# End of the spectral ffn: the last back-transform with two places at a time in the two halves of TensorE's array

## The chip, the cores and the metric

The kernel runs on one core of a Trainium2 chip. Its time is device microseconds of one execution. The kernel before was timed three times: 2250.99, 2252.79 and 2252.90 us, median 2252.79 us. The profile shows one such execution, with a span of 2251.2 us and a mean granted TensorE clock of 0.991.

## The reference, cut to what matters

The program computes two layers on a feature map `x` of 2 batches, 128 channels and 64 x 64 positions. Layer 0 is neighbourhood attention with a small feed-forward part. Layer 1 is global attention over 4096 tokens, and then a spectral ffn with a residual. The change lies at the very end of that ffn:

```python
def _stu_conv(phi, u, n):                     # causal convolution with K = 16 filters
    U_plus = irfft(Vf[None, :, :, None] * rfft(u)[:, :, None, :])[:, :sl]
    ...
def _compute_spectral(u, sigma, phi, Mpp, Mpm):
    out = einsum('btkd,k,kde->bte', U_plus, s, Mpp)
    out = out + einsum('btkd,k,kde->bte', U_minus, s, Mpm)
...
t = t + _L1_ffn_ref(_ln_t(t), ...)            # the residual
x = _from_tokens(t, x)                        # output: batch, channel, position
```

The kernel does the convolutions block by block in a frequency domain. At the end the spectrum of each result must go back to positions, and the residual `t` must be added.

## The kernel before, in words

Everything is float32. The ffn uses blocks of 256 positions; a block's transform has 320 real coefficients, which are 160 bins of 2 (`BINS` = 160). For each group of `GB` = 4 bins, `group()` multiplies inputs with filters (L1299: a contraction of 64 rows, alternately in rows 0 to 63 and 64 to 127 of the array, copied out by VectorE and ScalarE at L1300). `project()` contracts the result with 32 matrices of 128 x 128 (L1311), and ScalarE copies the finished accumulator to the spectrum tile `ob` (L1317). There are 40 such groups.

`ob` has channels on its partitions. Along the free dimension it has parity (2), batch (2), place `f` inside a stride of 8 (`FB` = 8), bin (160) and real or imaginary part (2). A "place" here is one combination of batch, parity and `f`: 2 x 2 x 8 = 32 places. The way back to positions takes each place apart:

- The bins are cut into chunks of 64, 64 and 32, so a chunk has 128, 128 and 64 coefficients.
- `turn()` transposes a place's coefficients by TensorE into PSUM (L1327, tile `pt`), so that coefficients lie on partitions, and ScalarE copies them to `t` (L1329).
- `back()` multiplies them with the inverse transform `inv` (L1338, tile `py`), contracting over the coefficients: 128 rows for chunks 0 and 1, 64 rows for chunk 2.
- For chunks 0 and 1, `back_into()` adds the result to `xa`, the residual in channel-major layout, by VectorE (L1350). These steps are slipped between the projections of later groups: TensorE's order in that loop is written by hand (`manual_schedule`).
- Chunk 2 is complete only after the last group, so it is done behind the loop. A list `last` holds 16 entries: half `h` of the positions, batch, parity and four places starting at `f0`. For each entry TensorE does four transposes and four back-multiplications, one entry's transposes ahead of the previous entry's multiplication, and VectorE adds `xa` and writes the output tile `o` (L1386). Each `o` holds one batch and one half of the positions, 1 MB; it is stored by one DMA of the sync queue (L1390). There are four, and `o` has two buffers.

The two halves `h` use the same coefficients with different columns of `inv`, so in this version every place is transposed twice. All PSUM tiles of this part (`pc`, `pt`, `py`) come from one ring of six buffers, `ps_c`.

Of the kernel before, what the change touches and what calls it, by code (L numbers as in the profile page):

```python
# [8 lines left out]
F32 = mybir.dt.float32  # L9
AF = mybir.ActivationFunctionType  # L10
ALU = mybir.AluOpType
# [3 lines left out]
P = 128  # L15
NB = 2
T = 4096
TH = T // 2
# [62 lines left out]
CB, FB, SG = 256, 8, 4  # L81
SB = CB // SG
NC = CB + SB

CHUNKS = (0, 1, 4, 5, 2, 3, 6, 7)
BINS = NC // 2
GB = 4
LG = 2 * FB
GROW = 4 * LG * KF


@with_exitstack
def kernel(
# [16 lines left out]
    nc = tc.nc  # L110
# [12 lines left out]
    xa = [xp.tile([P, T], F32, tag=f"xa{b}", name=f"xa{b}") for b in range(NB)]  # L123
# [15 lines left out]
    ident = const.tile([P, P], F32, name="ident")  # L139
# [79 lines left out]
    with l0a:  # L219
# [64 lines left out]
        for r in range(QT):  # L284
            lo = 6 - min(r, 6)
            src = bass.AP(
                rpb_pad.tensor, (RPR + r - 6) * RPW + 50, [[1, QT], [RPW, (HEADS - 1) * RPR - r // 7], [1, NTAB]]
            )
            rows_ = rev[r * QT : (r + 1) * QT].rearrange("p h n m -> p (h n) m")
# [979 lines left out]
    with ExitStack() as cv:  # L1269
        cp = cv.enter_context(tc.tile_pool(name="conv", bufs=5))  # L1270
        obp = cv.enter_context(tc.tile_pool(name="ob", bufs=1))
        ps_c = cv.enter_context(tc.tile_pool(name="ps_c", bufs=6, space=PSUM))
        ps_p = cv.enter_context(tc.tile_pool(name="ps_p", bufs=2, space=PSUM))

        ob = obp.tile([P, 2, NB, FB, BINS, 2], F32, name="ob")

        def inputs(q):

            ut = cp.tile([P, NB, 2, P], F32, tag="ut", name="ut")
            nc.sync.dma_start(  # L1280
                out=ut.rearrange("p b s d -> p (b s d)"),
                in_=us[2 * q : 2 * q + 2].rearrange("g i r f b s d -> (g i r f) (b s d)"),
            )
            return ut

        def group():


            y = cp.tile([P, 8, KF, 2, 32], F32, tag="y", name="y", bufs=2)
            for q in range(GB // 2):  # L1290
                ct, ut = ahead.pop(0)
                for par in range(2):

                    cv_ = ct[:, :, 0 : 288 + par * 32].rearrange("p o (l c) -> p o l c", l=2)[:, :, :, 0 : FB * KF]
                    for b in range(NB):
                        for f in range(2):
                            fp = slice(f * 64, (f + 1) * 64)
                            pc = ps_c.tile([P, 2, 2, FB * KF], F32, tag="pc", name="pc")
                            nc.tensor.matmul(pc, lhsT=ut[fp, b, par, :], rhs=cv_[fp], start=True, stop=True)  # L1299
                            (nc.scalar.copy if f else nc.vector.tensor_copy)(  # L1300
                                y[:, 4 * f : 4 * f + 4, :, par, b * 2 * FB + q : (b + 1) * 2 * FB : 2],
                                pc.rearrange("p r l (t k) -> p (r l) k t", k=KF),
                            )
                if to_load:
                    q_ = to_load.pop(0)
                    ahead.append((blocks(q_), inputs(q_)))
            return y

        def project(g, y, acc, l, k):

            nc.tensor.matmul(  # L1311
                acc, lhsT=(mmi if l else mpl)[:, k, :], rhs=y[:, 1::2, k, ::-1, :] if l else y[:, 0::2, k, :, :],
                start=(l == 0 and k == 0), stop=(l == 1 and k == KF - 1),
            )
            if l == 1 and k == KF - 1:
                ov = ob.rearrange("p s b t g r -> p (s b t) (g r)")[:, :, g * GB * 2 : (g + 1) * GB * 2]
                nc.scalar.copy(  # L1317
                    ov.rearrange("p m (q x) -> p x m q", q=2), acc.rearrange("p (x m q) -> p x m q", x=4, q=2)
                )

        def turn(chunk, b, par, f0, n):

            bn = min(64, BINS - chunk * 64)
            pt = ps_c.tile([P, n, P], F32, tag="pc", name="pt")
            for j in range(n):
                src = ob[:, par, b, FB - 1 - f0 - j, chunk * 64 : chunk * 64 + bn, :]
                nc.tensor.transpose(pt[0 : 2 * bn, j, :], src.rearrange("p g r -> p (g r)"), ident)  # L1327
            t = cp.tile([P, 4, P], F32, tag="t", name="t", bufs=2)
            nc.scalar.copy(t[0 : 2 * bn, 0:n, :], pt[0 : 2 * bn])  # L1329
            return t  # L1330

        def back(chunk, t, n, h):

            bn = min(64, BINS - chunk * 64)
            c0, cn = (0, CB) if h is None else (h * P, P)
            py = ps_c.tile([P, n, cn], F32, tag="pc", name="py")
            for j in range(n):
                nc.tensor.matmul(  # L1338
                    py[:, j, :], lhsT=t[0 : 2 * bn, j, :], rhs=inv[0 : 2 * bn, chunk, c0 : c0 + cn],
                    start=True, stop=True,  # L1340
                )
            return py

        def back_into(chunk, b, par, f0):

            t = turn(chunk, b, par, f0, 2)
            yield True
            py = back(chunk, t, 2, None)
            xv = xa[b][:, par * TH : (par + 1) * TH].rearrange("p (h f c) -> p f h c", h=2, f=FB)[:, f0 : f0 + 2]
            nc.vector.tensor_tensor(xv, py.rearrange("p f (h c) -> p f h c", h=2), xv, ALU.add)  # L1350
            yield None

        places = [(b, par, f0) for b in range(NB) for par in range(2) for f0 in range(0, FB, 2)]
        to_load = list(range(BINS // 2))
        ahead = [(ct, inputs(to_load.pop(0))) for ct in first_blocks]
        rest = []
        with tc.manual_schedule(engines={mybir.EngineType.PE}):
            y = group()
            for g in range(BINS // GB):
                following = group() if g + 1 < BINS // GB else None  # L1360
                acc = ps_p.tile([P, 64 * GB], F32, tag="acc", name="acc")
                for l in range(2):
                    for k in range(KF):
                        project(g, y, acc, l, k)
                        if rest and k in ((3, 11) if g >= 128 // GB else (7,)):
                            if next(rest[0], None) is None:
                                rest.pop(0)
                y = following
                if (g + 1) * GB in (64, 128):
                    rest += [back_into(g * GB // 64, *p) for p in places]  # L1370
            for steps in rest:
                for _ in steps:
                    pass


        last = [(h, b, par, f0) for h in range(2) for b in range(NB) for par in range(2) for f0 in range(0, FB, 4)]
        ahead = [turn(2, *last[0][1:], 4)]
        for i, (h, b, par, f0) in enumerate(last):
            if i + 1 < len(last):
                ahead.append(turn(2, *last[i + 1][1:], 4))  # L1380
            if par == 0 and f0 == 0:
                o = cp.tile([P, P, FB, 2], F32, tag="o", name="o", bufs=2)
            xv = xa[b][:, par * TH + h * (TH // 2) : par * TH + (h + 1) * (TH // 2)]
            xv = xv.rearrange("p (f c) -> p c f", f=FB)
            py = back(2, ahead.pop(0), 4, h)
            nc.vector.tensor_tensor(  # L1386
                o[:, :, f0 : f0 + 4, par], py.rearrange("p f c -> p c f"), xv[:, :, f0 : f0 + 4], ALU.add
            )
            if par == 1 and f0 + 4 == FB:
                nc.sync.dma_start(out=outf[b, :, h * TH : (h + 1) * TH], in_=o.rearrange("p c f r -> p (c f r)"))  # L1390


# [19 lines left out]
def _transforms():  # L1412

    import numpy as np

    f = np.arange(BINS)[None, :]
    real = (f == 0)

    def parts(n):
        n = np.arange(n)[:, None]
        a = 2 * np.pi * ((f * n) % NC) / NC
        return np.cos(a), -np.sin(a), (1.0 - 2.0 * (n % 2)) + 0.0 * f

    def pack(*cols):
        return np.stack(cols, axis=-1).reshape(cols[0].shape[0], -1).astype(np.float32)

    c, m, alt = parts(SB)
    seg = pack(c, np.where(real, alt, m))  # L1430
    c, m, alt = parts(CB)
    filters = pack(c, np.where(real, 0.0, m), np.where(real, 0.0, -m), np.where(real, alt, c))
    back = np.zeros((3 * P, CB), np.float32)
    back[0:NC] = pack(np.where(real, 1.0, 2.0 * c) / NC, np.where(real, alt, 2.0 * m) / NC).T
    return np.concatenate([seg, seg]), filters, back


# [49 lines left out]
```

## Time and profile before

| what | value |
|---|---|
| median time | 2252.79 us |
| span of the profile | 2251.2 us |
| TensorE busy | 2183.3 us, 97% of the span |
| VectorE busy | 939.8 us, 42% |
| ScalarE busy | 783.8 us, 35% |
| last projection ends, last projection copied out | 2217.7 us, 2218.3 us |
| last VectorE addition ends | 2245.9 us |
| transposes in the tail (128 x 64 weights) | 64, 279 ns each |
| back-multiplications in the tail (64 x 128 weights) | 128 instructions, 284 ns each |
| additions in the tail (L1386) | 16, 1042 ns each |

A matmul in float32 appears as two instructions in the trace, so the 64 calls of `back()`'s matmul in the tail are 128 instructions; a transpose is one. [...]consecutive instructions overlap. So the distance from start to start, which the chain of waits shows as time per group, is what an instruction costs TensorE, and the mean duration is not.

"64*128" after a TensorE instruction is the part of the array that its weights fill: 64 rows and 128 columns.

### The profile page before, as it was taken

The numbers are of one execution on the slowest core, as the hardware profiler recorded it, in microseconds if no ns is written. First come the engines' busy times: TensorE is split into PE (matmuls) and PEld (weight loads), VectorE is DVE, ScalarE is ACT, GpSimd is POOL, SyncE is SP. The second block draws the span as 40 slices with busy tenths as digits, with TensorE's granted clock in tenths as the row PEclk, the third lists the DMA queues.
The fourth block names the chain that finished last, engine by engine and source line by source line (L and its number), as shares of the span: only waits on it lengthen the run. The fifth ranks groups of instructions, "written<-read, shape, count | busy, mean of one in ns | idle before, by whom it ended". The sixth has DMA issues, their size and how long they took to land.

```text
span 2251.2 us, 31746 instructions
## 1 busy us (share of the span) xinstructions
PE 2183.3 (97%) x11908; PEld 1352.2 (60%) x11908; DVE 939.8 (42%) x3047; ACT 783.8 (35%) x1911; POOL 276.8 (12%) x354
## 2 busy tenths in 40 slices
PE   5899998999999999999999999999999999999998
PEld 3677765544445444444544447677677776767677
DVE  4799985433344336533233342222222323232323
ACT  2789883222333233222222332322322223232322
POOL 3367874200000000000000000000000000000000
PEclk8999998999999999999999999999999999999999
DMA  4222213011100016100000122212212122221101
GB/s 115 67 62 61 61 52 51 0 47 61 38 24 6 19 47 177 43 24 10 15 24 24 47 84 64 53 44 58 54 44 58 40 57 44 54 50 47 43 7 75
DMA packets 180858, 109.76 MB, mean 49 GB/s; under 512 B 32225, under 2 KB 165857, under 8 KB 180194
## 3 DMA queue, kind: packets, MB, share of 16 engines
q1 hardware_dynamic: 177866, 105.47, 17.9%
q10 hardware_dynamic: 2840, 2.27, 0.4%
q8 instruction: 94, 1.54, 0.3%
q14 instruction: 58, 0.48, 0.1%
HBM read 73.09 MB, written 34.60 MB: 48 GB/s over the span
## 4 chain that ended last, share of the span: by engine, by line
PE 85%; DVE 6%; POOL 3%; DMA 3%; ACT 1%; issue 1%; SPq 1%; DVEq 0%; ACTq 0%; POOLq 0%
PE acc L1311 25%; PE pc L1299 13%; PE bank L896 9%; PE own L924 9%; PE other L949 8%; PE bank L910 4%; PE py L1338 2%; PE bank L331 2%; PE bank L188 2%; PE bank L541 1%; PE bank L1041 1%; PE bank L1009 1%; PE bank L1150 1%; DMA st<-in_m_minus_dram 1%; PE po L563 1%
## 5 line engine op out<-in xcount | busy, mean ns | idle before, releaser
L1300 DVE COPY y<-pc 128x512 f32<-128x512 f32 x320 | 221.5, 692 | 351.5 <-PE pc L1299 347.8
L903 ACT ACTIVATE e<-bank 128x512 f32<-128x512 f32 x288 | 171.9, 597 | 558.9 <-PE bank L896 426.6
L896 PE MATMUL bank<-cm 128*128 128x512 f32 x576 | 298.4, 602 | 1.4 <-DVE y L652 1.4
L1311 PE MATMUL acc<-y,mpl 128*128 128x256 f32 x1280 | 292.1, 382 | 0.0
L1311 PE MATMUL acc<-y,mmi 128*128 128x256 f32 x1280 | 288.0, 379 | 0.0
L1299 PE MATMUL pc<-ct,ut 64*128 64x512 f32 x1280 | 285.2, 595 | 0.9 <-issue 0.9
L1311 PEld LDWEIGHTS acc<-y,mpl 128*128 128x128 f32 x1280 | 238.1, 190 | 59.4 <-issue 29.6
L1311 PEld LDWEIGHTS acc<-y,mmi 128*128 128x128 f32 x1280 | 242.6, 190 | 32.7
L1300 ACT COPY y<-pc 128x512 f32<-128x512 f32 x320 | 204.3, 638 | 87.4 <-PE pc L1299 87.4
L924 PE MATMUL own<-et,tok 128*128 128x512 f32 x448 | 227.2, 594 | 1.9 <-DVE part L913 1.9
L949 PE MATMUL other<-e,tok 128*128 128x512 f32 x448 | 228.6, 592 | 0.0
L913 DVE CUSTOM_DVE_ANT_0 et<-bank,one 128x512 f32<-128x512 f32 x224 | 145.7, 688 | 166.7 <-PE bank L910 166.6
L1299 PEld LDWEIGHTS pc<-ct,ut 64*128 64x128 f32 x1280 | 121.5, 187 | 145.8 <-issue 140.6
L1317 ACT COPY ob<-acc 128x256 f32<-128x256 f32 x40 | 23.8, 595 | 431.2 <-PE acc L1311 431.2
L924 PEld LDWEIGHTS own<-et,tok 128*128 128x128 f32 x448 | 84.3, 190 | 110.4 <-issue 72.4
L949 PEld LDWEIGHTS other<-e,tok 128*128 128x128 f32 x448 | 85.0, 190 | 106.6 <-issue 106.2
L896 PEld LDWEIGHTS bank<-cm 128*128 128x128 f32 x576 | 96.5, 193 | 73.3 <-issue 44.9
L1350 DVE TENSOR_TENSOR xa<-py,xa 128x512 f32<-128x512 f32 x32 | 22.2, 692 | 281.4 <-PE py L1338 281.4
L910 PEld LDWEIGHTS bank<-ident,e 128*128 128x128 f32 x896 | 103.4, 141 | 55.1 <-issue 47.2
L160 POOL TENSOR_TENSOR ln_rs<-ln_rs,mhalf 128x4 f32<-128x4 f32 x24 | 24.3, 1010 | 857.8 <-DVE ln_rs L159 857.8
L528 ACT ACTIVATE p<-p,mn 128x196 f32<-128x196 f32 x256 | 114.4, 449 | 21.6 <-DVE mn L518 13.9
L910 PE MATMUL bank<-ident,e 128*128 128x128 f32 x896 | 116.9, 273 | 0.0
(200 smaller groups left out, 2335.7 us busy)
## 6 DMA issues: line engine op xcount, KB each, us to landing
ut<-us SPq DMA_DIRECT2D x80, 256.0 KB
us<-ub SPq DMA_DIRECT2D x64, 256.0 KB
vw<-vd SPq DMA_DIRECT2D x256, 49.0 KB
ct<-gs SPq DMA_DIRECT2D x160, 72.0 KB
ct<-gs SPq DMA_DIRECT2D x160, 64.0 KB
gs<-ub SPq DMA_DIRECT2D x20, 256.0 KB
vd<-v SPq DMA_DIRECT2D x128, 32.0 KB
st<-in_m_plus_dram SPq DMA_DIRECT2D x16, 256.0 KB
```

Source lines behind the costliest of these rows:

```text
L188: nc.tensor.transpose(ps[:, j * P : (j + 1) * P], src[:, j, :], ident)
L331: nc.tensor.matmul(pl, lhsT=wg[:, lo : lo + P], rhs=zT, start=True, stop=True)
L528: nc.scalar.activation(p, p, AF.Exp, bias=t[name + "mn"][:, h : h + 1], scale=-1.0, accum_out=t["den"][:, u, h : h + 1],)
L896: nc.tensor.matmul(ps, lhsT=cm[b][:, n * P : (n + 1) * P], rhs=cm[b][:, chunk(c)], start=True, stop=True)
L903: nc.scalar.activation(e, ps, AF.Exp, bias=0.0, scale=ASCALE, accum_out=part[:, n, c : c + 1])
L910: nc.tensor.transpose(pt[:, k * P : (k + 1) * P], es[k][:, m * P : (m + 1) * P], ident)
L913: nc.vector.tensor_tensor_reduce(et, pt, one, 1.0, 0.0, ALU.mult, ALU.add, part[:, n, a : a + 1])
L924: nc.tensor.matmul(own, lhsT=tok[b][:, n, :], rhs=e, start=first, stop=last)
L949: nc.tensor.matmul(other, lhsT=tok[b][:, 4 * CHUNKS[a] + j, :], rhs=es[j], start=(j == 0), stop=(j == 3))
L1299: nc.tensor.matmul(pc, lhsT=ut[fp, b, par, :], rhs=cv_[fp], start=True, stop=True)
L1300: (nc.scalar.copy if f else nc.vector.tensor_copy)(y[:, 4 * f : 4 * f + 4, :, par, b * 2 * FB + q : (b + 1) * 2 * FB : 2], pc.rearrange("p ...
L1311: nc.tensor.matmul(acc, lhsT=(mmi if l else mpl)[:, k, :], rhs=y[:, 1::2, k, ::-1, :] if l else y[:, 0::2, k, :, :], start=(l == 0 and k = ...
```

## The change

The chunk of 64 coefficients fills only half of the array's rows. The change puts the transposed coefficients of two places into one tile, one place in rows 0 to 63 and the other in rows 64 to 127, and multiplies both at the same time, each in its half of the array.

- The last 32 bins get a spectrum tile of their own, `ob_last`, in which two neighbouring places lie side by side: 2 x 32 x 2 = 128 contiguous numbers. One transpose of 128 x 128 turns two places. All 16 transposes run ahead of the multiplications, once, and both halves `h` use their results; four `t` tiles hold them, so `t` gets four buffers where it had two.
- The rows of `inv` for chunk 2 are stored twice, so that rows 64 to 127 hold the same matrix as rows 0 to 63.
- The multiplications alternate between the two halves of the array, into two PSUM tiles, `odd` and `even`.
- For the even places TensorE also adds the residual: a multiplication of `xa` with the identity matrix starts the accumulation, and ScalarE copies the sum to `o`. For the odd places VectorE adds the residual as before.
- `turn()` and `back()` are folded into `back_into()`, which does for chunks 0 and 1 what it did.

```diff
-        ob = obp.tile([P, 2, NB, FB, BINS, 2], F32, name="ob")
+        ob = obp.tile([P, 2, NB, FB, 2 * BC, 2], F32, name="ob")
+        ob_last = obp.tile([P, 2, NB, FB, BINS - 2 * BC, 2], F32, name="ob_last")
...
-                ov = ob.rearrange("p s b t g r -> p (s b t) (g r)")[:, :, g * GB * 2 : (g + 1) * GB * 2]
+                o_, g0 = (ob, g * GB) if g * GB < 2 * BC else (ob_last, g * GB - 2 * BC)
+                ov = o_.rearrange("p s b t g r -> p (s b t) (g r)")[:, :, g0 * 2 : (g0 + GB) * 2]
...
-            t = cp.tile([P, 4, P], F32, tag="t", name="t", bufs=2)
+            t = cp.tile([P, 4, P], F32, tag="t", name="t", bufs=4)
...
-        last = [(h, b, par, f0) for h in range(2) for b in range(NB) for par in range(2) for f0 in range(0, FB, 4)]
-        ahead = [turn(2, *last[0][1:], 4)]
-        for i, (h, b, par, f0) in enumerate(last):
-            if i + 1 < len(last):
-                ahead.append(turn(2, *last[i + 1][1:], 4))
...
-            py = back(2, ahead.pop(0), 4, h)
-            nc.vector.tensor_tensor(
-                o[:, :, f0 : f0 + 4, par], py.rearrange("p f c -> p c f"), xv[:, :, f0 : f0 + 4], ALU.add
-            )
+        turned_ = {}
+        for b in range(NB):
+            for par in range(2):
+                pt = ps_c.tile([P, 4, P], F32, tag="pc", name="pt")
+                for i in range(4):
+                    src = ob_last[:, par, b, 2 * i : 2 * i + 2]
+                    nc.tensor.transpose(pt[:, 3 - i, :], src.rearrange("p m g r -> p (m g r)"), ident)
+                turned_[b, par] = cp.tile([P, 4, P], F32, tag="t", name="t", bufs=4)
+                nc.scalar.copy(turned_[b, par], pt)
+        for h in range(2):
+            for b in range(NB):
+                o = cp.tile([P, P, FB, 2], F32, tag="o", name="o", bufs=2)
+                for par in range(2):
...
+                    odd, even = (ps_c.tile([P, 4, P], F32, tag="pc", name="py") for _ in range(2))
+                    nc.tensor.matmul(even, lhsT=ident, rhs=xv[:, 0::2], start=True, stop=False)
+                    for i in range(4):
+                        for q, py in ((0, odd), (1, even)):
+                            rows_ = slice(q * 64, (q + 1) * 64)
+                            nc.tensor.matmul(
+                                py[:, i, :], lhsT=turned_[b, par][rows_, i, :], rhs=inv[rows_, 2, h * P : (h + 1) * P],
+                                start=(q == 0), stop=(q == 0 or i == 3),
+                            )
+                    nc.scalar.copy(o[:, :, 0::2, par], even.rearrange("p f c -> p c f"))
+                    nc.vector.tensor_tensor(
+                        o[:, :, 1::2, par], odd.rearrange("p f c -> p c f"), xv[:, 1::2].rearrange("p f c -> p c f"), ALU.add
+                    )
                 nc.sync.dma_start(out=outf[b, :, h * TH : (h + 1) * TH], in_=o.rearrange("p c f r -> p (c f r)"))
...
+    back[NC:] = back[2 * P : NC]
```

More of the change, by code (lines that the diff above doesn't have):

```diff
@@ L87 @@
 GB = 4
+BC = 64
 LG = 2 * FB
@@ L1319, in project @@
                 )
[L1321 to L1327, printed above, removed]
-            t = cp.tile([P, 4, P], F32, tag="t", name="t", bufs=2)
[L1329 to L1340, printed above, removed]
-                )
-            return py
-        def back_into(chunk, b, par, f0):
-            t = turn(chunk, b, par, f0, 2)
+        def back_into(chunk, b, par, f0):
+            pt = ps_c.tile([P, 2, P], F32, tag="pc", name="pt")
+            for j in range(2):
+                src = ob[:, par, b, FB - 1 - f0 - j, chunk * BC : (chunk + 1) * BC, :]
+                nc.tensor.transpose(pt[:, j, :], src.rearrange("p g r -> p (g r)"), ident)
+            t = cp.tile([P, 4, P], F32, tag="t", name="t", bufs=4)
+            nc.scalar.copy(t[:, 0:2, :], pt)
             yield True
-            py = back(chunk, t, 2, None)
+            py = ps_c.tile([P, 2, CB], F32, tag="pc", name="py")
+            for j in range(2):
+                nc.tensor.matmul(py[:, j, :], lhsT=t[:, j, :], rhs=inv[:, chunk, :], start=True, stop=True)
             xv = xa[b][:, par * TH : (par + 1) * TH].rearrange("p (h f c) -> p f h c", h=2, f=FB)[:, f0 : f0 + 2]
@@ L1364 @@
                         project(g, y, acc, l, k)
-                        if rest and k in ((3, 11) if g >= 128 // GB else (7,)):
+                        if rest and k in ((3, 11) if g >= 2 * BC // GB else (7,)):
                             if next(rest[0], None) is None:
@@ L1368 @@
                 y = following
-                if (g + 1) * GB in (64, 128):
-                    rest += [back_into(g * GB // 64, *p) for p in places]
+                if (g + 1) * GB in (BC, 2 * BC):
+                    rest += [back_into(g * GB // BC, *p) for p in places]
             for steps in rest:
@@ L1373 @@
                     pass
-        last = [(h, b, par, f0) for h in range(2) for b in range(NB) for par in range(2) for f0 in range(0, FB, 4)]
-        ahead = [turn(2, *last[0][1:], 4)]
-        for i, (h, b, par, f0) in enumerate(last):
-            if i + 1 < len(last):
-                ahead.append(turn(2, *last[i + 1][1:], 4))
-            if par == 0 and f0 == 0:
-                o = cp.tile([P, P, FB, 2], F32, tag="o", name="o", bufs=2)
-            xv = xa[b][:, par * TH + h * (TH // 2) : par * TH + (h + 1) * (TH // 2)]
-            xv = xv.rearrange("p (f c) -> p c f", f=FB)
-            py = back(2, ahead.pop(0), 4, h)
-            nc.vector.tensor_tensor(
-                o[:, :, f0 : f0 + 4, par], py.rearrange("p f c -> p c f"), xv[:, :, f0 : f0 + 4], ALU.add
-            )
-            if par == 1 and f0 + 4 == FB:
+        turned_ = {}
@@ new lines @@
+        for b in range(NB):
[8 more added lines that the diff above has]
+            for b in range(NB):
+                o = cp.tile([P, P, FB, 2], F32, tag="o", name="o", bufs=2)
+                for par in range(2):
+                    xv = xa[b][:, par * TH + h * (TH // 2) : par * TH + (h + 1) * (TH // 2)]
+                    xv = xv.rearrange("p (f c) -> p f c", f=FB)
+                    odd, even = (ps_c.tile([P, 4, P], F32, tag="pc", name="py") for _ in range(2))
[11 more added lines that the diff above has]
+                    )
```

## The prediction

> **What bounds the kernel now.** I read four views. The first is the page's chain of waits by engine and line, to see which engine sets the end:
>
> ```profile
> PE 85%; DVE 6%; POOL 3%; DMA 3%; ACT 1%; issue 1%; SPq 1%; DVEq 0%; ACTq 0%; POOLq 0%
> ```
>
> TensorE is the bound. The change touches only work behind the loop of groups, so the second view is the same chain for that stretch alone (columns: start, time on the chain, engine, tile and line, instructions):
>
> ```profile
> 2217.75 0.59 ACT ob L1317
> 2218.34 0.04 issue
> 2218.39 0.64 PE pt L1327 x4
> ...
> 2219.74 1.16 PE py L1338 x8
> 2220.89 0.56 PE pt L1327 x4
> 2221.45 1.08 PE py L1338 x8
> 2222.54 0.56 PE pt L1327 x4
> ...
> 2242.80 1.10 PE py L1338 x8
> 2243.90 0.02 issue
> 2243.92 1.04 DVE o L1386
> 2244.97 0.94 DVEq L1483
> ```
>
> The reader is to see one unbroken alternation: four transposes, 0.56 us, then eight back-multiplication instructions, 1.08 us. Sixteen entries of 1.64 us are 26.2 us, all TensorE. Only the last additions and the last store (from 2245.9 to the span's end at 2251.2, 5.3 us) follow. The third view is the waits in the tail (engine and line, what it waited for, total, times, longest):
>
> ```profile
> ACT t L1329 <- PE pt L1327: 16.0, 15, 1.4
> DVE o L1386 <- PE py L1338: 12.6, 15, 4.2
> ```
>
> ScalarE and VectorE wait for TensorE there, so what TensorE saves shortens the program until one of them takes more per step. The fourth view shows what this kernel's trace has of the new pattern. In the attention stage, four instructions of 64 rows and 512 columns in alternating halves (L1009) stand between pairs of full-array instructions of 512 columns (L896); this is that stretch of the chain:
>
> ```profile
> 1196.83 0.86 PE bank L896 x2
> ...
> 1198.66 1.06 PE bank L1009 x4
> 1199.72 1.05 PE bank L896 x2
> 1200.77 1.06 PE bank L1009 x4
> 1201.83 1.05 PE bank L896 x2
> ```
>
> Undisturbed, two full-array instructions take 0.86 us, 0.43 each. Four half-array ones take 1.06, not 1.72: two run at a time. Each change between full and half array costs about 0.2 us: 1.06 - 0.86 = 0.20 on one side, 1.05 - 0.86 = 0.19 on the other.
>
> [...] The tail's second-last and last blocks run without a change between them, and sixteen instructions take 2.05 us where eight take 1.16: 0.111 us each[...].
>
> **The change, part by part.**
>
> *Transposes.* Removed: 64 at 0.56 us per four, sixteen times. Added: 16 of 128 x 128, two places each. The nearest row is the loop's own 128 x 128 transposes, 0.22 us for two on the chain, 0.109 each. The first four take 0.64 as now (they wait for the same copy of the last accumulator, which ends at 2218.34, and start at 2218.39); twelve more take 1.31: 1.95 us, to 2220.34.
>
> *Copies of the transposes.* Four instead of sixteen, by the 64 x 512 row 0.58 us each. The first can start at 2219.1, as now, so all four are done by 2221.5. The first multiplication needs the first copy (done at 2219.7) and comes at about 2221.3; each later one comes 2 us after its predecessor. On no path: the transposes hide the first copy, and multiplications the rest. Had it to wait for all four, 0.4 us would be lost.
>
> *Identity multiplication.* Added: eight calls of 128 x 512, two instructions each, 0.86 us. From the half array back to the full one it is 1.05, like L896 above; the first follows transposes in the full array, 0.95.
>
> *Back-multiplications.* The same 64 calls, 128 instructions, but in eight blocks of sixteen, alternating halves. If two run at a time, a block is eight slots. A slot is 128 columns: L1009's slots of 512 columns take 0.43, and a quarter of that is 0.107[...]; I take the measured 0.112 of one half running alone. A block is 8 x 0.112 + 0.20 for the change = 1.10 us.
>
> *A step* is so 1.05 + 1.10 = 2.15 us for what took two entries, 3.28 us, before. Eight steps: 2220.34 + 0.95 + 1.10 + 7 x 2.15 = 2237.4, where the last addition can start. Most of the saved time is transposes; the identity multiplication gives back 8 x 0.86 = 6.9 us of it.
>
> *Evictions.* Per step VectorE does one addition of 128 x 512 instead of two. Its form is new (it now writes every fourth number), but it reads the same transposed PSUM order, so 1.04 us as L1386; the bounds are 0.69 (L1350, straight) and 1.04. ScalarE copies 128 x 512 reordered: straight it is 0.58 (L1329); the reordered copy of half the size at L1317 takes 0.59, so at most 1.19. Both lie beside 2.15 us of TensorE. Behind them nothing else queues: the next copy or addition, and the store of `o`. The ring of six PSUM buffers holds three steps of two, so TensorE waits only for evictions of three steps ago, over 4 us old. Only the last eviction is on the path: 1.04, at most 1.19.
>
> *Stores.* Four of 1 MB, as before. They are issued every 4.3 us instead of 6.6, and the last takes under 4 us from issue to landing (issued at 2245.93, everything ended by 2251.2). So the third `o` finds its buffer free: its first write comes three steps, 6.4 us, after the first `o`'s store is issued. The last store ends as it did, 5.3 us after the last addition.
>
> *At nothing:* `ob_last`, the doubled rows of `inv` and four `t` buffers. The copy at L1317 has the same size, and only its distance from place to place changes; the DMA of `inv` has the same size; the loop's order on every engine stays as it was.
>
> *Sum.* The last addition ends at 2237.4 + 0.02 + 1.04 = 2238.5 instead of 2245.9: 7.4 us less, so **2252.8 - 7.4 = 2245.4 us**.
>
> **The rivals.**
>
> *Half the overlap (2250).* Loads of 187 ns (the mean of a 64 x 128 load in the tail) might not hide behind streams of only 107, since L1299 and L1009 have streams of 430 to hide them. A slot of 0.187 adds 8 x 0.075 = 0.6 us a step, 4.8 in all. Against it: 0.111 us per instruction in one half alone already hides them.
>
> *No overlap (2252, no change).* Sixteen instructions at 0.111 in turn add 0.89 us a step, 7.1 in all. It speaks for it that halves with streams this short do not run together anywhere in this trace with 128 columns of weights; against it the loop's L1299, 16 calls of 64 rows in alternating halves, whose 32 instructions of 512 columns take 7.07 us on the chain, 0.22 each instead of 0.43.
>
> *Slower (2258).* Without overlap, and with half of a mode's change, 0.1 us, at each of the seven changes of half inside a block: 5.6 us more. L1299's 0.22 us per instruction leaves no room for it.
>
> A wait of TensorE for the evictions as new bound would need over 2.15 us for a copy that the trace bounds at 1.19.
>
> **How the numbers follow.** Overlap as forecast 0.89, half 0.04, none 0.04, slower 0.03. A change under 0.2%, 4.5 us, counts as none: half and no overlap fall there, 0.08. The range is that of the first case: timing of the kernel itself spreads over 1.9 us, the terms of a step (switches, slot) are good to 0.1 us each, 0.8 over eight steps, and copies and the last eviction to -0.35 and +0.5. That gives 2243.5 to 2247.7 and leaves the rivals, 0.11, out.
>
> **What would show it.** In the profile after: the chain from the last copy of an accumulator is 16 transposes in about 1.9 us, then eight times an identity block of about 1.05 and a back-multiplication block of about 1.1; VectorE and ScalarE wait for TensorE in each step; the last addition starts about 7 us earlier than now. A back-multiplication block of 2 us would mean no overlap; TensorE waiting for the new ScalarE copy (line 1388 of the changed kernel) or the new addition (1389) would mean that the evictions bind; a store that waits for another would show as a wait ahead of the third `o`.

## The result, and the profile after

The changed kernel takes 2246.6 us (median of six runs, 2243.97 to 2248.43) where the kernel before, timed beside it, takes 2252.85 us (six runs, 2250.99 to 2255.06). The ratio is 0.997, with a 95% interval of 0.9957 to 0.9983: 6 us faster, between 4 and 10. The forecast was 2245.4 us, with a range of 2243.5 to 2247.7.

The measure of this study is the **tail**: from the end of ScalarE's copy of the last accumulator to the end of the last eviction into `o`. Outside the tail the kernels hardly differ: in all twelve profiles of this study the loop, from its first multiplication of the filters to its last copy, takes 878.12 us, and only the moment at which it starts differs, from 1338.9 to 1347.2 us. So the tail says more than the whole time. Before, it ran from 2218.34 to 2245.90, 27.56 us. This is the chain of waits of the changed kernel in the same stretch (start, time on the chain, engine, tile and line, instructions). In its code L1370 transposes, L1380 multiplies with the identity, L1384 multiplies with `inv`, and L1388 and L1389 are the evictions by ScalarE and VectorE; the variants below number the same lines a little differently.

```profile
2219.09 0.59 ACT ob_last L1320
...
2219.72 1.97 PE pt L1370 x16
2221.69 0.86 PE py L1380 x2
2222.55 1.09 PE py L1384 x16
...
2236.53 1.05 PE py L1380 x2
2237.58 1.14 PE py L1384 x16
...
2238.75 1.09 ACT o L1388
```

The alternation of 0.56 and 1.08, sixteen times, has become one block of 16 transposes and then 1.05 and 1.09, eight times. The tail runs from 2219.68 to 2238.75 + 1.09 = 2239.84, 20.16 us, so it is 7.40 us shorter. The rest of the program is as it was: from the last eviction to the end of the span, 5.3 us in both.

The tail's groups by line and shape (busy time, mean ns of one; then idle time before them and its releaser) show what changed on all three engines. The first line is the kernel before, the others are the changed kernel:

```profile
L1338 PE MATMUL py<-inv,t 64*128 64x128 f32 x128 | 18.2, 284 | 0.3 <-ACT t L1329 0.3
L1384 PE MATMUL py<-inv,t 64*128 64x128 f32 x128 | 9.3, 285 | 0.0
L1380 PE MATMUL py<-xa,ident 128*128 128x512 f32 x16 | 8.9, 638 | 0.0
L1388 ACT COPY o<-py 128x512 f32<-128x512 f32 x8 | 8.8, 1100 | 8.5 <-PE py L1384 8.5
L1389 DVE TENSOR_TENSOR o<-py,xa 128x512 f32<-128x512 f32 x8 | 8.8, 1099 | 13.0 <-PE py L1384 13.0
```

The 128 back-multiplication instructions keep their mean of 284 to 285 ns, but their busy time falls from 18.2 us to 9.3: each now lies on top of another. Both evictions wait for TensorE in all eight steps (8.5 and 13.0 us), so TensorE is still the bound.

### The profile page after: what moved, and what is told of

Same layout as the page of the kernel before. It is cut to its first block, busy times and chain, and to the rows that moved or that the text cites. A ratio compares the mean times of both kernels' runs of the same rounds, so it can differ in the third digit from the quotient of the medians.

```text
span 2245.2 us, 31634 instructions
## 1 busy us (share of the span) xinstructions
PE 2178.7 (97%) x11876; PEld 1344.8 (60%) x11876; DVE 931.9 (42%) x3039; ACT 787.0 (35%) x1907; POOL 277.2 (12%) x354
## 4 chain that ended last, share of the span: by engine, by line
PE 86%; DVE 6%; POOL 3%; DMA 2%; ACT 1%; issue 1%; SPq 1%; ACTq 0%; POOLq 0%; DVEq 0%
PE acc L1313 25%; PE pc L1301 13%; PE own L925 9%; PE bank L897 9%; PE other L950 8%; PE bank L911 4%; PE bank L332 2%; PE bank L189 2%; PE bank L542 2%; PE bank L1010 1%; PE bank L1042 1%; PE py L1335 1%; PE bank L1151 1%; DMA st<-in_m_minus_dram 1%; PE bank L506 1%; PE po L564 1%
```

## The experiments

All tails are read from one profile of each kernel; ratios are to the kernel before on the same chip, with 95% intervals.

| kernel | tail, us | ratio |
|---|---|---|
| before | 27.56 | 1 |
| changed | 20.16 | 0.997 (0.9957 to 0.9983) |
| e1: halves in turn | 24.49 | 0.9985 (0.9978 to 0.9991) |
| e2: turned twice | 21.87 | 0.9964 (0.9952 to 0.9975) |
| e3: VectorE adds all | 21.03 | 0.9971 (0.9958 to 0.9984) |
| e4: turned once alone | 21.67 | 0.9973 (0.996 to 0.9985) |
| e5: straight reading | 20.10 | 0.9968 (0.9956 to 0.998) |
| e6: identities in pairs | 18.68 | 0.9964 (0.9951 to 0.9977) |
| e7: VectorE adds all, four `o` | 18.72 | 0.9965 (0.9951 to 0.9979) |
| e8: a quarter by TensorE, four `o` | 15.54 | 0.9943 (0.9931 to 0.9955) |
| e9: two by two | 20.91 | one run |
| e10: straight writing | 20.06 | one run |

The whole times agree with the tails only within their intervals, because the start of the loop moves them by more than most of the variants do. e2, for example, has a longer tail than the changed kernel, and about the same ratio.

### e1: is it the pairing?

```diff
-                    for i in range(4):
-                        for q, py in ((0, odd), (1, even)):
+                    for q, py in ((0, odd), (1, even)):
+                        for i in range(4):
```

> The changed kernel with one thing altered: in each step all four multiplications of rows 0 to 63 are issued first, and then all four of rows 64 to 127, instead of alternately. Instructions, tiles and evictions are the same. 'Tail' is the time from the end of the last accumulator's copy to the end of the last eviction: 27.6 us before, 20.2 us in the changed kernel. Theory (the gain needs two halves running together[...]): a block of sixteen takes 16 x 0.111 + 0.20 = 1.98 us instead of 1.09, the tail grows by 8 x 0.89 = 7.1 to 27.3 us, and the time is about 2253 us, as before the change. Rival (TensorE pairs instructions of the two halves however far apart they stand): blocks stay at 1.1 us, tail 20.2, time 2246 us.

The chain in the tail of e1:

```profile
2228.19 1.64 PE py L1384 x16
2229.83 1.05 PE py L1380 x2
```

A block takes 1.64 us: neither side was right. The same instructions, only in another order, cost 0.55 us more per step, 4.3 us in the tail, so the overlap of the halves is a real part of the gain and depends on the order. But it isn't all lost. With 0.20 us for the change of mode, 1.64 us are 13 slots of 0.11, where full overlap has 8 and none 16: three slots of the second half fit beside the end of the first. The single records of a block agree: the second half's first instruction starts 0.56 us into it, 6 ns after the fifth of the first half, when three of the first half's eight are still waiting. So in this order instructions of the free half started ahead of three earlier ones of the other half.

### e9: how far ahead?

```diff
-                    for i in range(4):
-                        for q, py in ((0, odd), (1, even)):
+                    for i, q, py in (
+                        (0, 0, odd), (1, 0, odd), (0, 1, even), (1, 1, even),
+                        (2, 0, odd), (3, 0, odd), (2, 1, even), (3, 1, even),
+                    ):
```

> The changed kernel with the halves taken two by two: two multiplications of rows 0 to 63, two of rows 64 to 127, and so on. It sizes what e1 showed: with four and four, the second half started when the first had three of its eight instructions left, and a block took 1.64 us, neither 1.98 (no overlap) nor 1.09 (full). Theory (TensorE starts an instruction of the free half if no more than three matmul instructions of the busy half stand before it): the second half starts one slot late, a block is 1.09 + 0.11 = 1.2 us and the tail 20.2 + 8 x 0.11 = 21.1 us. Rival (overlap comes only at a seam between halves, some 0.33 us at each, as in e1): three seams overlap about three slots each, less than all, a block of 1.1 to 1.2 us as well but with the second half starting two slots late or more and gaps between the pairs.

A block in the chain of e9:

```profile
2231.21 1.19 PE py L1387 x16
```

The size is as forecast, 1.19 us, but the slot is not lost where the theory put it. In the records of all eight blocks the second half starts 13 ns after the first, with three matmul instructions of the first half waiting ahead of it. The loss comes at the seam in the middle. The second half's fourth weight load starts 0.34 us into the block and its fifth only at 0.55, where 0.45 would be one slot later: that is just after the first half's fifth instruction has started, at 0.55, and again left three waiting. In e1 the second half starts at the same moment. So the theory's count agrees with the records of both orders: at 0.56 us in e1, and at 0.01 and 0.55 us in e9, an instruction of the free half starts with three matmul instructions of the busy half waiting ahead of it, and none of these starts with four. What the theory had wrong is the start, where only three of the four are waiting. Why it is three was not shown.

e9 shows one thing more, which the changed kernel does not: VectorE waits for a store.

```profile
DVE o L1392 <- DMA out_dram<-o: 1.6, 1, 1.6
```

The wait is not on the path: the tail, 20.91 us, is longer than the changed kernel's by about the eight slots (8 x 0.10 us), and no more.

### e2: undo "turned once"

```diff
-        for b in range(NB):
-            for par in range(2):
-                pt = ...                           # four transposes, one copy
-        for h in range(2):
+        for h in range(2):
+            for b in range(NB):
+                for par in range(2):
+                    pt = ...                       # the same, for each half again
```

> The changed kernel with one part undone: the 16 transposes of the last chunk and their four copies are done again ahead of the second half of the positions. Theory (TensorE's time is the tail): 16 x 0.109 = 1.75 us more, tail 21.9 us, time about 2248.3 us. Rival (the copies of the second set queue behind evictions on ScalarE and hold up the multiplications): up to four copies of 0.6 us in addition, tail 24.3 us.

The chain of e2 at the start of the second half of the positions:

```profile
2228.95 1.90 PE pt L1371 x16
2230.85 0.86 PE py L1380 x2
```

The second set takes 1.90 us, 0.16 more than 16 x 0.109, and after it the identity multiplication needs 0.86 instead of 1.05: the change of mode now falls on the transposes. The net is 1.71 us, near the first theory's 1.75. The four copies queue on ScalarE without holding TensorE up.

### e4: "turned once" alone

```diff
-        ahead = [turn(2, *last[0][1:], 4)]
-        for i, (h, b, par, f0) in enumerate(last):
-            if i + 1 < len(last):
-                ahead.append(turn(2, *last[i + 1][1:], 4))
+        turned = {p[1:]: turn(2, *p[1:], 4, ...) for i, p in enumerate(last[: len(last) // 2])}
+        for h, b, par, f0 in last:
...
-            py = back(2, ahead.pop(0), 4, h)
+            py = back(2, turned[b, par, f0], 4, h)
```

> The kernel before with one part of the change alone: the last chunk's transposes are done once, ahead, for both halves of the positions (32 of 128 x 64 instead of 64); no pairing of places, no residual by TensorE. Theory: 0.64 + 28 x 0.109 = 3.7 us of transposes, then sixteen blocks of eight without a change of mode, 0.89 us each on TensorE against 1.04 us on VectorE, so VectorE becomes the bound: 3.7 + 1.1 + 16 x 1.04 = 21.4 us of tail instead of 27.6, and the time is about 2246.7 us: most of the gain of the whole change. Rival (pairing brings most of it, and turning once only the 32 transposes saved, 4.5 us, at unchanged blocks of 1.08 us): 23.1 us of tail, 2248.4 us.

From the chain in the tail of e4:

```profile
2221.87 3.68 PE pt L1327 x32
2225.55 1.10 PE py L1338 x8
...
2230.65 5.01 DMA out_dram<-o
```

The tail is 21.67 us: 5.9 of the change's 7.4 us come from this part alone, and they come in two ways. Half the transposes go, and with them the changes of mode between the blocks. The chain then leaves TensorE for VectorE (L1384), and it shows something that I had not expected: the third output tile waits for the first store, which takes 5.01 us here (VectorE's wait for it is 1.3 us). The additions make up for it, since they follow each other every 0.94 to 0.98 us when VectorE has work waiting, although one lasts 1.04. This part and the pairing of e1 don't add up to the gain (5.9 and 4.3 us make more than 7.4): alone, turning once moves the bound to VectorE, and in the whole change the identity multiplications take back most of what the pairing saves.

### e3 and e7: without the residual on TensorE

```diff
-                    nc.tensor.matmul(even, lhsT=ident, rhs=xv[:, 0::2], start=True, stop=False)
...
-                    nc.scalar.copy(o[:, :, 0::2, par], even.rearrange("p f c -> p c f"))
+                    nc.vector.tensor_tensor(
+                        o[:, :, 0::2, par], even.rearrange("p f c -> p c f"), xv[:, 0::2].rearrange("p f c -> p c f"), ALU.add
+                    )
```

> The changed kernel without the identity multiplications: VectorE adds the residual for even and odd places alike, ScalarE evicts nothing. Theory (the residual by TensorE is a load taken from VectorE and not a gain by itself): TensorE needs only 8 x 0.9 us and no changes of mode, but VectorE then has 16 additions of 1.10 us, and becomes the bound: 1.97 + 1.1 + 16 x 1.10 = 20.7 us of tail, 0.5 more than the changed kernel, time about 2247 us, with TensorE waiting for VectorE. Rival (TensorE remains the bound): 1.97 + 0.2 + 7.2 + 2.2 = 11.6 us of tail, time about 2238 us.

The waits in the tail of e3 (engine and line, what it waited for, total, times, longest), and the store on its chain:

```profile
PE py L1383 <- DVE o L1387: 3.7, 5, 2.2
DVE o L1387 <- DMA out_dram<-o: 2.3, 1, 2.3
```

```profile
2229.42 5.99 DMA out_dram<-o
```

TensorE now waits for VectorE, and the tail is 21.03 us, near the first theory's 20.7. The size is luck in part, since two errors cancel: the additions start every 0.95 to 0.98 us and not every 1.10, and VectorE waits 2.3 us for a store, 5.99 us from issue to release. e7 takes that wait away, with four output tiles in the space of `y`, which is free by then:

```diff
-                o = cp.tile([P, P, FB, 2], F32, tag="o", name="o", bufs=2)
+                o = store[:, 2 * h + b]
...
+        store = cp.tile([P, 4, P, FB, 2], F32, tag="y", name="o", bufs=2)
```

> e3 (VectorE adds the residual everywhere) with one thing more: four output tiles instead of two, in a buffer that is free by then, so that no addition waits for a store. In e3 the first addition of the third tile stood 2.3 us behind the first store. Theory (that wait and VectorE's additions, 0.95 us apart when they follow each other, are what made e3's 21.0 us): 1.97 + 1.1 + 16 x 0.95 + 0.1 = 18.4 us of tail, less than the changed kernel's 20.2. Rival (the additions slow down while a store reads the same memory, or the stores queue): 20 us or more.

The tail falls to 18.72 us, and no engine waits for a store any more. So the residual on TensorE brings 0.9 us (21.03 to 20.16) where there are two output tiles, and costs 1.4 us (20.16 against 18.72) where there are four. For the second figure the changed kernel was not run with four tiles; it waits for no store with two, so more of them should not change its tail, but that is argued and not shown.

### e6: what the changes of mode cost

```diff
+                evens = []
+                for par in range(2):
+                    ...
+                    evens.append(ps_c.tile([P, 4, P], F32, tag="pc", name="py"))
+                    nc.tensor.matmul(evens[par], lhsT=ident, rhs=xv[:, 0::2], start=True, stop=False)
                 for par in range(2):
...
-                    nc.tensor.matmul(even, lhsT=ident, rhs=xv[:, 0::2], start=True, stop=False)
```

> The changed kernel with the identity multiplications of both parities issued together, ahead of their two blocks of back-multiplications: as many instructions, but four visits to the half-array mode instead of eight. Theory (each visit costs 0.2 us on entering and 0.2 us on leaving, all of it on TensorE's path): four visits fewer, 4 x 0.4 = 1.6 us, tail 18.6 us, time 1.6 us below the changed kernel's. Rival (the changes of mode hide behind weight loads, or the PSUM ring of six holds TensorE up with four tiles in use): tail 20.2 us or more.

Two blocks and two identity multiplications in the chain of e6:

```profile
2222.90 1.99 PE py L1389 x32
2224.89 1.91 PE py L1381 x4
```

Two blocks in one visit take 1.99 us instead of 2 x 1.09, and two identity multiplications 1.91 instead of 2 x 1.05. That is 0.38 us for each visit saved, and 1.48 us in the tail: the changes of mode lie on the path, and four tiles in use at a time did not make TensorE wait for the ring of six PSUM buffers (its matmuls of L1381 and L1389 stand idle for 0.0 us).

### e5 and e10: which side of the eviction costs

```diff
-                    nc.scalar.copy(o[:, :, 0::2, par], even.rearrange("p f c -> p c f"))
+                    nc.scalar.copy(o[:, :, 0::2, par].rearrange("p c f -> p f c"), even)
```

and the same for the addition. In e10 it is the other way round: `o` is written in straight runs, and PSUM is read with its stride. The output of e10 then lies in another order than the reference's, so it is a measurement and not a kernel to use.

```diff
-                    nc.scalar.copy(o[:, :, 0::2, par], even.rearrange("p f c -> p c f"))
+                    oc = o.rearrange("p c f r -> p (c f r)")[:, par * 1024 : (par + 1) * 1024]
+                    nc.scalar.copy(oc[:, 0:512].rearrange("p (c f) -> p c f", f=4), even.rearrange("p f c -> p c f"))
...
```

> The changed kernel with the loops of the last evictions exchanged: PSUM is read in the order in which it lies, and the output tile is written with a stride of 64 bytes, instead of reading PSUM with a stride of 512 bytes and writing with one of 16. The same numbers go to the same places. It asks which side of the reordered eviction costs: 128x512 takes 1.10 us on either engine, and a straight ScalarE copy of that size 0.60 (the transposes' copies). Theory A (the strided reading of PSUM): evictions 0.6 to 0.7 us, the tail 0.4 us shorter, 19.7 us. Theory B (the strided writing of SBUF): evictions stay at 1.1 us, tail 20.2 us. Either way the time is near the changed kernel's, since only the last eviction is on the path.

> The changed kernel with the last evictions writing straight runs of 512 numbers, while PSUM is still read with a stride of 512 bytes. The output then lies in another order than the reference's. With e5, where the reading was straight and the writing strided and an eviction still took 1.05 us, it tells the two sides apart. Theory (the strided writing of SBUF is what costs): ScalarE's eviction falls to about 0.6 us, its straight copy's time, VectorE's to about 0.7, and the tail by 0.4 to 0.5 us, to 19.7. Rival (either side alone costs the same): evictions stay at 1.05 to 1.1 us.

The evictions of e5, and then those of e10 (count, then minimum, median and maximum in ns, first and last start):

```profile
L1389 DVE TENSOR_TENSOR o<-py,xa x8: 1021/1048/1081, 2221.6 to 2236.6; 128x512 f32<-128x512 f32 x8
L1388 ACT COPY o<-py x8: 1028/1054/1086, 2221.6 to 2236.7; 128x512 f32<-128x512 f32 x8
```

```profile
L1390 DVE TENSOR_TENSOR o<-py,xa x8: 1028/1044/1049, 2223.6 to 2238.7; 128x512 f32<-128x512 f32 x8
L1389 ACT COPY o<-py x8: 586/586/588, 2223.7 to 2238.7; 128x512 f32<-128x512 f32 x8
```

For ScalarE it is the writing: 1054 ns with straight reading, 586 with straight writing. For VectorE either side alone is enough: 1048 and 1044 ns, against 692 for the addition of the loop (L1350 before), which reads and writes runs of 128. In e10 it reads `xa` with a stride as well as PSUM, and no run tells the two apart. So the tail gains next to nothing (20.10 and 20.06 us).

### e8: a version that beats both

TensorE adds the residual, and ScalarE evicts, for the even places of the second parity only; there are four output tiles as in e7.

```diff
-                    nc.tensor.matmul(even, lhsT=ident, rhs=xv[:, 0::2], start=True, stop=False)
+                    if par:
+                        nc.tensor.matmul(even, lhsT=ident, rhs=xv[:, 0::2], start=True, stop=False)
...
+                    if par:
                         nc.scalar.copy(o[:, :, 0::2, par], even.rearrange("p f c -> p c f"))
+                    else:
+                        nc.vector.tensor_tensor(o[:, :, 0::2, par], even.rearrange("p f c -> p c f"), ...)
```

> The changed kernel rebalanced: TensorE adds the residual, and ScalarE evicts, for the even places of the second parity only (a quarter of the places), VectorE adds it for the other three quarters, and there are four output tiles. TensorE: 1.97 us of transposes, then four identity blocks of 1.05 and eight blocks of 0.9 with five entries into the half-array mode, 12.4 us; VectorE: twelve additions, 11.4 us, beside it; the last eviction 1.1. Theory (whichever of the two engines takes longer in this stretch is the tail): 15.5 us of tail instead of 20.2, and a time about 11 to 12 us below the kernel before. Rival (stores, each 4 to 6 us from issue to landing, now come every 3.1 us and pile up behind each other): the last store lands 2 to 3 us later than 5.3 us after the last eviction, and the gain on the kernel before is 9 us.

The chain in the tail of e8:

```profile
2219.08 1.09 PE py L1386 x16
2220.17 1.05 PE py L1382 x2
2221.22 1.99 PE py L1386 x32
...
2231.51 1.09 ACT o L1391
```

The tail is 15.54 us, against 15.5 forecast, and the kernel takes 2239.86 us (five runs) against 2252.89 before on the same chip, a ratio of 0.9943 (0.9931 to 0.9955). Of these 13.0 us the tail explains 12.0. The stores do not pile up: the span ends 5.5 us after the last eviction, where it was 5.3.

## Why the prediction was right

*The bound and the path.* TensorE's time behind the loop was the tail, and what it saved came off the end: forecast 7.4 us, measured 7.40. That mechanism was right, and the agreement to a hundredth is luck: the first identity multiplication took 0.86 us and not 0.95, because it follows transposes without a change of mode, while the last block took 1.14 and not 1.10 and the last eviction 1.09 and not 1.04.

*Transposes.* Forecast 1.95 us for sixteen, measured 1.97. e2 confirms the price of one, 0.11 us. "Most of the saved time is transposes" is true only of the net. In the forecast's own terms they save 7.0 us (16 x 0.56 less 1.95) and the pairing 8.5 us (16 x 1.08 less 8 x 1.10), and the identity multiplications with their changes of mode give back 8.3 (0.95 and 7 x 1.05): nearly all that the pairing saves. It is from these that e6, e7 and e8 gained more.

*Two at a time.* Forecast 1.10 us for a block, measured 1.09. The rivals "half the overlap", "no overlap" and "slower" needed blocks of 1.7, 1.98 and 2.7 us. That the halves did run together is shown by e1, where the order alone takes 4.3 us of it back. Weight loads that last 187 ns in the records did not stand in the way: instructions of one half start 112 ns apart, each load beside the instruction ahead of it. In every kernel here the two halves write to PSUM tiles of their own; what one tile for both would do was not shown.

*Identity and mode.* Forecast 1.05 us, measured 1.05. The price of a change of mode, 0.19 to 0.20 us in the attention stage, held in the tail (1.05 less 0.86 is 0.19), and e6, with half of the visits, saved 0.38 us for each visit less. The records show where the 0.19 us lie. At a step of the changed kernel the first full-array load starts 0.20 us after the last half-array instruction, which is 0.09 more than the usual 0.11; and the second identity instruction starts 0.53 us after the first instead of 0.43, another 0.10. There the first load starts 1 to 2 ns ahead of its own instruction; that of the first identity multiplication, which follows transposes, starts 107 ns ahead.

*Evictions.* The step said 1.04 us for VectorE, with 0.69 and 1.04 as bounds, and 0.58 to 1.19 for ScalarE. Measured were 1.10 for both. VectorE's lies 0.06 us outside its bound; ScalarE's ended last, 1.09 us, and moved the sum by 0.05. Both stayed beside TensorE, as forecast. That either stride alone makes VectorE slow, and the writing ScalarE, came only with e5 and e10.

*Stores.* No eviction of the changed kernel waits for a store, as forecast, but both figures behind that were wrong. "Under 4 us from issue to landing" was read from the last store, with no other behind it; the first store of the changed kernel took 4.6 us. And the third tile's first write came 5.3 us after that store's issue, not 6.4: three steps were counted, and the eviction that has to end before the store was left out. The margin was 0.8 us, not 2.4. The first store took 6.0 us in e3, 5.0 in e4 and 5.9 in e9, and VectorE waited 2.3, 1.3 and 1.6 us. In e9 the steps are even longer than in the changed kernel, so that this profile shows no wait is partly luck.

*The whole.* The median is 1.2 us above the forecast and inside the range. The tail agrees with its forecast and the loop takes the same 878.12 us in both profiles; it only starts later, at 1340.2 us before and at 1341.5 after, behind work that the change leaves alone. Why that stretch varies was not studied. The range allowed 1.9 us for it, from three executions; the 28 of the kernel before that were timed beside e1 to e4 spread over 7.0 us (2251.27 to 2258.30), and the slowest of the changed kernel's six, 2248.43 us, lies above the range. So the tail was forecast, and that the median of the whole fell so near is partly luck.

## What to carry to other kernels

Where TensorE is the bound of a stretch, price an edit from start to start on the chain, not by mean durations, and take the price of a change of array mode from a stage of the same trace that has one (here 0.19 to 0.20 us in the attention stage, and 0.19 in the tail). Give independent matmuls of 64 rows to the two halves alternately: issued in runs of four calls, the same instructions overlapped by less than half (three slots of eight, 1.64 us a block against 1.09). And when a residual can be added on either of two engines, split it so that both end together, and give the stores enough tiles: that was worth more here (20.2 to 15.5 us of tail) than moving half of it.

## What the runs showed of the hardware

- A block of sixteen half-array instructions took 1.09 us with the calls alternating (the changed kernel), 1.19 two by two (e9) and 1.64 four by four (e1). In e1 the second half started 0.56 us into the block, and in e9 0.01 us, each time with three instructions of the first half waiting ahead of it.
- Each visit to the half-array mode saved in e6 shortened the chain by 0.38 us, entering and leaving together. In the changed kernel the first weight load after each change starts 1 to 2 ns ahead of its own instruction, and the next instruction of that part of the array comes 0.10 us later than usual (0.21 us and not 0.11 on entering, 0.53 and not 0.43 on leaving).
- ScalarE's copy of 128 x 512 takes 0.59 to 0.60 us with straight writes, whether PSUM is read straight (L1372) or with a stride (e10), and 1.06 (e5) to 1.13 (e6) in the mean with writes 16 or 64 bytes apart. VectorE's addition takes 1.04 (e10) to 1.10 (the changed kernel) in the mean if the reading or the writing is strided, and 0.69 if neither is (L1350).
- VectorE's additions of 1.03 to 1.11 us start 0.94 to 0.99 us apart when there is always one waiting (e3, e4, e7).
- The last store of 1 MB landed 3.9 us after its issue, before and after the change; the first took 4.6 us in the changed kernel and 5.0 to 6.0 in e3, e4 and e9. Why they differ was not studied.
